# Where the background pieces of an attention stream stand within a step: behind the scores, or beside the sums of values

## The chip, the cores and the metric

The kernel runs on one NeuronCore of one Trainium2 chip. The metric is the device time of one execution in microseconds (us); lower is better. The core has engines that run side by side and each take their instructions in the order in which they were issued: TensorE (PE; its weight loads are listed as PEld), VectorE (DVE), ScalarE (ACT), GpSimd (POOL), and SyncE (SP), which here issues all DMA transfers. They wait for each other through semaphores. TensorE writes its products to PSUM, a memory of eight banks, from where VectorE and ScalarE fetch them.

## The reference

Two transformer blocks are applied in a row to `x` of 2048 tokens and 256 features, with 16 heads of 16. Cut to what matters:

```
def layer0(x, ...):                       # x0, x1: the two halves of the tokens
    x0 = x0 + gate * mha(mod(ln(x0)))     # attention inside each half   (stage 0)
    x1 = x1 + gate * mha(mod(ln(x1)))
    ox = attend(q(x0), k(x1), v(x1))      # each half looks at the other (stage 1)
    oy = attend(q(x1), k(x0), v(x0))
    x = x + gate * proj(ox, oy)
    x = x + gate * mlp(mod(ln(x)))        # 256 -> 1024 -> 256, tanh-gelu
def layer1(x, memory, mask):
    x = layernorm(x + mha(x, x, x, mask))         # 2048 x 2048 mask     (stage 2)
    x = layernorm(x + mha(x, memory, memory))     # 1601 context tokens  (stage 3)
    x = layernorm(x + relu(x @ w1 + b1) @ w2 + b2)
def attend(q, k, v):
    return softmax(q @ k.T / 4) @ v
```

## The kernel before

**Stages, units, steps.** The four attentions are four stages, and `stream` runs them as one long sequence. A stage has four blocks of 512 queries, a block four groups of four heads. One block and one group is a unit (in stage 2 the first block is cut in two parts, by keys). A unit goes over its keys in tiles of 128 with two head pairs for each, so it has two steps for every key tile: 16 steps a unit in stages 0 and 1 (1024 keys), 32 in stage 2 (16 in its first block's eight units), 26 in stage 3 (1601 keys). That makes 1440 steps. Stage 2 alone has a mask; its steps are called masked.

**What one step issues.** Four things, each on TensorE and then on another engine:
- *maxima* (`take_maxima`, `maxima`, L839): queries times keys for a unit ahead, to find each query's largest score; VectorE reduces them (L854, masked L847). There is about one such pair in a step, placed by due times (`todo`). When a unit's maxima are complete, `negated` and three steps later `as_rows` (L878, copied by ScalarE in L883) turn them into rows.
- *scores* (`second[s2]()`, which is `pair` in `weights_of`): keys times queries (L917), less the maxima (L924), in stage 2 with the mask added by a product with the identity (L932). ScalarE then takes exp of the 128 x 1024 scores (L937, the tile `e`).
- *sums* (`f()`, which is `add` in `values_of`, L953): `e` of some steps ago times the values, accumulated over a whole unit in one PSUM bank.
- *background* (`after(step)`): what is due of `later` (among it `as_rows`, `invert`, `divide`), mask tiles turned by TensorE in stage 2 (`mask_columns`, L805, copied by ScalarE in L810), one waiting transfer of keys or values, and one advance of the first background chain.

**Background chains.** All the rest of the network (projection, normalization, transposes, queries, keys, values, MLP) is written as generators, one chain for every block and stage, which advance a bit in each step. Work on TensorE is cut into pieces (`piece`): a first function issues a product into a PSUM bank, and the last one copies the result out of it. `after` starts the product. The copy is issued by `before()`, at the start of the next step:

```
if unfinished and background and not background[0][2] and background[0][1] <= now[0]:
    if not advance(background[0]):
```

In the same call the chain comes to its next piece, whose product `after` then starts in that step. So a run of pieces issues one product in each step, and every copy is issued one step after its product. Which engine copies depends on the kind of piece:

- transposes (`transposed`, L343): ScalarE (L354 or L358)
- queries and keys (`halves`, L385): ScalarE makes `hi` (L392), then VectorE `lo` (L393), which needs `hi`
- MLP up (L514): ScalarE (L522)
- values (L415), projection (L459), MLP down (L534): VectorE (L425, L477, L489)

The gelu of stage 1's MLP is taken in the first down product (L533, eight ScalarE instructions), which waits for them.

**Banks.** Six of PSUM's eight banks are three double buffers for maxima and scores (`big_ps`). The other two are `m0` and `m1`, one buffer each (`one_ps`): one holds the unit's sums, the other (`small[0]`) takes all pieces, `as_rows` and `mask_columns` of that time. The two change roles at the third step of a unit (`s2 == 2`), when `copy_sums` has ScalarE copy the finished sums (L985).

**Order.** Nothing is reordered after the program: `tc.manual_schedule` keeps every engine's instructions as issued. In an unmasked step the order on TensorE is thus maxima, sums, scores, background; in a masked one maxima, scores, sums, background. TensorE works in different tile shapes: maxima and scores use 64 rows and 128 columns (`64*128` in the profile), sums `128*32`, the mask's product and all background work `128*128`. [...]

After the last step, the last block's chain runs alone (from about 3331 us on).

Of the kernel before, what the change touches and what calls it, by code (L numbers as in the profile page):

```python
# [66 lines left out]
def slot_rows(st, slot):  # L67
    return sum(key_rows(st, n) for n in KEYS[st][slot])


def slots_of(st, b):

    return ((b // 2,), (1 - b // 2,), (0, 1), (0, 1))[st]
# [3 lines left out]
def two_layers(ctx: ExitStack, tc: tile.TileContext, a: dict, out: bass.AP):  # L77
# [583 lines left out]
    def advance(entry):  # L661

        try:
            got = next(entry[0])
        except StopIteration:
            return False
        entry[2] = got is BANK
        if got is not BANK:
            entry[1] = now[0] + got
        return True  # L670
# [190 lines left out]
    def negated(u):  # L861

        neg = sb.tile([P, TPB, 2, 2], F32, tag="neg", bufs=2, name="neg")
        nc.vector.tensor_reduce(
            neg.rearrange("p t c i -> p (t c i)"),
            u["pm"].rearrange("p t c i n -> p (t c i) n"), AX.X, ALU.max, negate=True,
        )
        v = negpad.rearrange("p t (c x) -> p t c x", c=2)
        nc.vector.tensor_copy(v[:, :, :, 0:3:2], neg)
        nc.vector.tensor_tensor(  # L870
            v[:, :, :, 1:4:2], neg, v[:, :, :, 0:3:2].bitcast(F32), ALU.subtract
        )

    def as_rows(u):

        m = one_ps()
        for qt in range(TPB):
            nc.tensor.matmul(  # L878
                m[:, qt * P : (qt + 1) * P], lhsT=negpad[:, qt, :], rhs=identR,
                start=True, stop=True,  # L880
            )
        u["nm"] = sb.tile([P, BLK], F32R, tag="nm", bufs=2, name="nm")
        nc.scalar.copy(u["nm"], m)  # L883
        if "part" in u:

            t = sb.tile([P, 2, 4 * BLK // P], F32, tag="mh", bufs=2, name="mh")
            for j in range(4):
                for h in range(2):
                    r = 64 * (j // 2) + 2 * (j % 2) + h
                    nc.sync.dma_start(  # L890
                        t[PH * j : PH * (j + 1), h, :], u["nm"][r : r + 1, :].bitcast(F32)
                    )

            def add():
                n = u["minus"] = part_tile(u, "minus")
                nc.vector.tensor_tensor(n, t[:, 0, :], t[:, 1, :], ALU.add)

            later.append([4, add, False])
# [179 lines left out]
    def stream(stages):  # L1078

        units = []  # L1080
        for st in stages:
            for b in ORDER[st]:
                blocks[st, b] = {}
                if (st, b) == (2, SPLIT):
                    units += [
                        {"st": st, "b": b, "g": g, "slots": (slot,), "part": slot}
                        for slot in range(2) for g in range(NG)
                    ]
                else:
                    units += [  # L1090
                        {"st": st, "b": b, "g": g, "slots": slots_of(st, b)} for g in range(NG)
                    ]
        for i, u in enumerate(units):
            u["i"] = i

        columns: list = []
        at = 0
        for u in units:
            steps = [(slot, kt) for slot in u["slots"] for kt in range(-(-slot_rows(u["st"], slot) // P))]
            if u["st"] == 2 and u["g"] == 0:  # L1100
                columns += [
                    (at + 2 * n - COLUMNS, u["b"], slot, kt) for n, (slot, kt) in enumerate(steps)
                ]
            u["start"], u["steps"] = at, 2 * len(steps)
            at += 2 * len(steps)

        todo: list = []
        for u, w in zip(reversed(units), [*reversed(units[:-1]), None]):
            tiles = maxima(u)
            n = len(tiles)  # L1110
            begin, length = (w["start"], w["steps"]) if w else (-n, n)
            for k in range(n - 1, -1, -1):
                due = begin + k * length / n - AHEAD
                todo.append([min(due, todo[-1][0] - SPACING) if todo else due, u, tiles[k]])

        def take_maxima(step):
            while todo and todo[-1][0] <= step:
                _, u, f = todo.pop()
                f()
                if not todo or todo[-1][1] is not u:  # L1120
                    all_maxima(u)

        def all_maxima(u):
            negated(u)
            later.append([3, lambda: as_rows(u), True])
            if u.get("part") == 0 and u["g"] == NG - 1:
                waiting.append((2, 1, 1))

        def before():

            if unfinished and background and not background[0][2] and background[0][1] <= now[0]:
                if not advance(background[0]):
                    background.pop(0)

        def after(step):

            now[0] += 1
            due = [x for x in later if x[0] <= 0]
            later[:] = [[x[0] - 1, *x[1:]] for x in later if x[0] > 0]
            for x in due:  # L1140
                x[1]()
            turned = any(x[2] for x in due)
            while columns and columns[0][0] <= step:
                mask_columns(*columns.pop(0)[1:])
                turned = True
            load_ready()
            soon = any(x[0] <= 0 and x[2] for x in later)
            soon = soon or (columns and columns[0][0] <= step + 1)
            if background and background[0][1] <= now[0]:
                if not background[0][2] or not (turned or soon):  # L1150
                    if not advance(background[0]):
                        background.pop(0)

        streaming[0] = True
        for u in units[:2]:
            load_queries(u)
        for step in range(math.floor(todo[-1][0]), 0):
            small[0] = 1
            before()
            take_maxima(step)  # L1160
            after(step)
        pending: list = []
        step = 0
        for u in units:
            i = u["i"]
            masked = u["st"] == 2
            small[0] = i % 2
            second = weights_of(u)
            for s2 in range(len(second)):
                before()  # L1170
                if s2 == 3:
                    pending += values_of(u)
                if s2 == 1 and i + 2 < len(units):
                    load_queries(units[i + 2])
                take_maxima(step)
                f = pending.pop(0) if pending else None
                if f and not masked:
                    f()
                second[s2]()

                if f and masked:
                    f()
                after(step)
                step += 1
                if s2 == 2:
                    small[0] = (i + 1) % 2
                if s2 == 2 and i:
                    w = units[i - 1]
                    copy_sums(w)
                    part = w.get("part")  # L1190
                    if part is None:
                        later.append([3, lambda w=w: invert(w), False])
                        later.append([6, lambda w=w: divide(w), False])
                    elif part == 1:
                        v = units[i - 1 - NG]
                        later.append([3, lambda w=w, v=v: compare(w, v), False])
                        later.append([4, lambda w=w, v=v: invert_both(w, v), False])
                        later.append([7, lambda w=w: (fetch_first(w), divide(w)), False])
                    if w["g"] == NG - 1 and part != 0:
                        chain_after(w)  # L1200
        small[0] = len(units) % 2
        for f in pending:
            if f:
                f()
        for x in later:
            x[1]()
        flush((0, 1))
        streaming[0] = False
        w = units[-1]
        copy_sums(w)  # L1210
        invert(w)
        divide(w)
        chain_after(w)
        while background:
            if not advance(background[0]):
                background.pop(0)
        flush((None,))
# [90 lines left out]
```

## Time and profile before

| | us |
|---|---|
| median of the runs | 3405.08 (3401.45 to 3407.21) |
| the profiled execution | 3412.04 |
| its span, first to last instruction | 3410.2 |
| ScalarE busy with exp (L937, 1440 instructions) | 1467.0 |
| PE busy with sums (L953, 10432 records) | 907.7 |
| start of stage 2's first masked score, of its last | 1272.8, 2519.5 |

How to read it: "busy" is the time in which an engine has an instruction in work; the shares of a chain are those of the way that ended last, followed back from the end. A line such as `L514` is the kernel's line, and `m_ps<-hT,w_mlp` says that the tile `m_ps` is made from `hT` and `w_mlp`. PEclk is the share of its full clock that TensorE was granted. TensorE's ends are modelled, so a matmul's length overlaps with the next one; starts are the safer reading, and below, times of TensorE's work are taken from start to start.

### The profile page before, as it was taken

Reading aid. Unit: us, or ns where it says so; the run is one execution under the profiler, and the core shown is the slowest. Engines: PE = TensorE matmul, PEld = TensorE weight load, DVE = VectorE, ACT = ScalarE, POOL = GpSimd, SP = SyncE. Lnnn points to the kernel's source line nnn. Section 1 sums busy time; section 2 is a strip of 40 time slices with the busy share of each in tenths; the row PEclk is TensorE's granted clock in tenths of the full one; section 3 lists DMA queues with packets and bytes.
Section 4 is the critical chain, followed back from the end, with each engine's and each line's share of the span. In section 5 each row is a group of like instructions: output and inputs, shape, how many; then the busy total and the mean of one; then the engine's idle time right before and its main releaser. Section 6 shows DMA issues by size and latency. Waiting matters only on the chain.

```text
span 3410.2 us, 56623 instructions
## 1 busy us (share of the span) xinstructions
PE 3088.3 (91%) x22447; PEld 1360.9 (40%) x22592; DVE 2121.6 (62%) x3858; ACT 1712.8 (50%) x1868; POOL 404.1 (12%) x344
## 2 busy tenths in 40 slices
PE   4899999999999889798999999999999999999995
PEld 2334444444443434333333333333334444444433
DVE  2676766764646365366867777777656747657541
ACT  1365655655545445243555555554555646546461
POOL 0001101101010121204013011201000011110112
PEclk8899999999999999899999999999999999999997
DMA  6652152160205221443111001102241100000000
GB/s 183 152 91 62 43 109 64 57 120 22 65 18 111 34 87 33 111 93 108 30 46 51 14 23 53 39 17 53 46 85 49 26 10 26 25 18 26 10 14 16
DMA packets 162362, 191.20 MB, mean 56 GB/s; under 512 B 82584, under 2 KB 95520, under 8 KB 162096
## 3 DMA queue, kind: packets, MB, share of 16 engines
q1 hardware_dynamic: 162096, 187.57, 22.6%
q8 instruction: 178, 2.92, 0.4%
q14 instruction: 88, 0.72, 0.1%
HBM read 129.91 MB, written 48.46 MB: 52 GB/s over the span
## 4 chain that ended last, share of the span: by engine, by line
PE 72%; DVE 8%; ACT 7%; DMA 5%; issue 3%; SPq 3%; POOL 2%; ACTq 0%; DVEq 0%; POOLq 0%
PE m_ps L953 19%; PE s_ps L917 13%; PE s_ps L839 11%; PE s_ps L924 8%; PE s_ps L932 6%; ACT e L937 6%; PE m_ps L514 3%; PE m_ps L534 3%; DVE pm L854 3%; PE m_ps L385 2%; DVE s_ps L847 2%; PE m_ps L459 2%; PE m_ps L415 2%; PE m_ps L878 1%; DVE t L328 1%
## 5 line engine op out<-in xcount | busy, mean ns | idle before, releaser
L937 ACT ACTIVATE e<-s_ps 128x1024 f32<-128x1024 f32 (+1 forms) x1440 | 1467.0, 1024 | 1387.6 <-PE s_ps L924 794.2
L854 DVE TENSOR_REDUCE pm<-s_ps 128x2 f32<-128x1024 f32 (+3 forms) x1024 | 1120.4, 1106 | 533.0 <-PE s_ps L839 528.8
L953 PE MATMUL m_ps<-e,V 128*32 128x256 f32 (+2 forms) x10432 | 907.7, 419 | 10.3 <-DVE lo L393 4.5
L847 DVE CUSTOM_DVE_ANT_0 s_ps<-s_ps,bias 128x512 f32<-128x512 f32 x1024 | 713.0, 700 | 300.4 <-PE s_ps L839 166.8
L839 PE MATMUL s_ps<-kT,q 64*128 64x512 f32 (+3 forms) x3072 | 677.1, 444 | 121.3 <-ACT e L937 51.1
L917 PE MATMUL s_ps<-q,kT 64*128 64x512 f32 (+1 forms) x2880 | 677.1, 466 | 54.0 <-ACT e L937 28.4
L924 PE MATMUL s_ps<-nm,sel 64*128 64x512 f32 (+1 forms) x2880 | 575.1, 395 | 0.1
L839 PEld LDWEIGHTS s_ps<-kT,q 64*128 64x128 f32 x3072 | 293.7, 186 | 538.6 <-issue 313.8
L917 PEld LDWEIGHTS s_ps<-q,kT 64*128 64x128 f32 (+1 forms) x2880 | 270.4, 184 | 500.4 <-issue 241.7
L953 PEld LDWEIGHTS m_ps<-e,V 128*32 128x32 f32 (+1 forms) x10432 | 207.3, 108 | 437.6 <-issue 416.0
L1031 POOL TENSOR_TENSOR oT<-oT,rd_rows 64x512 f32<-64x512 f32 x64 | 81.6, 1275 | 1902.3 <-DMA rd_rows<-rd_dr 1448.3
L932 PE MATMUL s_ps<-biasT,ident 128*128 128x512 bf16 x879 | 278.5, 385 | 23.1 <-issue 23.1
L924 PEld LDWEIGHTS s_ps<-nm,sel 64*128 64x128 f32 (+1 forms) x2880 | 275.2, 187 | 12.0 <-ACT nm L883 0.8
L782 POOL TENSOR_SCALAR bias<-raw 128x512 bf16<-128x512 int32 x64 | 123.0, 1922 | 298.4 <-DMA raw<-in_mask 276.7
L847 DVE DVE_READ_ACCUMULATOR2_ANT pm<- 128x1 f32 x1024 | 144.8, 141 | 0.0
L932 PEld LDWEIGHTS <-ident 128*128 128x128 bf16 x1024 | 58.3, 97 | 187.3 <-issue 187.3
L393 DVE SCALAR_TENSOR_TENSOR lo<-m_ps,qkb,hi 128x512 fp32r<-128x512 f32 (+2 forms) x56 | 41.1, 734 | 140.9 <-ACT hi L392 99.0
L534 PE MATMUL m_ps<-w_mlp,hid 128*128 128x256 f32 x448 | 111.2, 404 | 11.9 <-ACT hid L533 11.9
L385 PE MATMUL m_ps<-hT,w_qk 128*128 128x512 f32 (+2 forms) x224 | 111.0, 619 | 9.9 <-DVE lo L393 9.2
L514 PE MATMUL m_ps<-hT,w_mlp 128*128 128x512 f32 x224 | 111.0, 618 | 0.7 <-ACT hT L354 0.7
L534 PEld LDWEIGHTS m_ps<-w_mlp,hid 128*128 128x128 f32 x448 | 87.2, 201 | 35.4 <-ACT hid L533 14.7
L392 ACT ACTIVATE hi<-m_ps,qkb 128x512 fp32r<-128x512 f32 (+2 forms) x56 | 37.7, 674 | 82.7 <-PE m_ps L385 58.1
(106 smaller groups left out, 1233.6 us busy)
## 6 DMA issues: line engine op xcount, KB each, us to landing
q<-q_dr SPq DMA_DIRECT2D x544, 64.0 KB
kT<-k_dr SPq DMA_DIRECT2D x192, 128.0 KB
raw<-in_mask SPq DMA_DIRECT2D x64, 256.0 KB
q_dr<-hi SPq DMA_DIRECT2D x32, 256.0 KB
q_dr<-lo SPq DMA_DIRECT2D x32, 256.0 KB
oT<-sums SPq DMA_DIRECT2D x256, 32.0 KB
rd_rows<-rd_dr SPq DMA_DIRECT2D x64, 128.0 KB
v_dr<-v SPq DMA_DIRECT2D x14, 544.0 KB
```

The lines of the kernel that those rows point to most:

```text
L385: nc.tensor.matmul(m[:, :n], lhsT=wqk[:, k, w, c, :], rhs=hT[:, k, :n], start=k == 0, stop=k == 1)
L514: nc.tensor.matmul(m, lhsT=w1[k][:, f * P : (f + 1) * P], rhs=hT[:, k, :], start=k == 0, stop=k == 1,)
L534: nc.tensor.matmul(m[:, q2 * D : (q2 + 1) * D], lhsT=hid[f][:, qt * P : (qt + 1) * P], rhs=w2[f // 4][:, f % 4, :], start=f == 0, stop=f = ...
L782: nc.gpsimd.tensor_scalar(bias_rows[b, slot, qt][:, j * BLK : (j + 1) * BLK], raw, 0.0, MASKED, ALU.is_equal, ALU.mult,)
L839: nc.tensor.matmul(s[:, h, :nn], lhsT=u["q"][64 * h : 64 * h + 64, i, qt * P : (qt + 1) * P], rhs=kT[g][slot][64 * h : 64 * h + 64, i, c : ...
L847: nc.vector.tensor_tensor_reduce(out=s[:, h, :], in0=s[:, h, :], in1=bias_rows[b, slot, qt][:, c : c + nn], scale=1.0, scalar=-3.0e38, op0 ...
L854: nc.vector.tensor_reduce(u["pm"][:, qt, :, i, n], s[:, :, :nn], AX.X, ALU.max)
L917: nc.tensor.matmul(s[:r, h, :], lhsT=kT[g][slot][64 * h : 64 * h + 64, i, kt * P : kt * P + r], rhs=u["q"][64 * h : 64 * h + 64, i, :], st ...
L924: nc.tensor.matmul(s[:r, h, :], lhsT=sel[64 * h : 64 * h + 64, i, :r], rhs=u["nm"][64 * h : 64 * h + 64, :], start=False, stop=not masked,)
L932: nc.tensor.matmul(s[:, h, :], lhsT=ident16, rhs=bias_columns[b, slot, kt], start=False, stop=True,)
L937: nc.scalar.activation(e[:r], s[:r], AF.Exp, scale=SCALE)
L953: nc.tensor.matmul(u["av"][PH * j : PH * (j + 1), cut], lhsT=V[g][slot][:r, kt * GW + j * VW : kt * GW + j * VW + PH], rhs=u["e"][n, j % 2 ...
```

## The change

Within a step, the calls change places; nothing else does. Unmasked, the background now comes ahead of the sums and scores; masked, it comes between the scores and the sums.

```diff
                 take_maxima(step)
                 f = pending.pop(0) if pending else None
-                if f and not masked:
+
+
+                if masked:
+                    second[s2]()
+                after(step)
+                if f:
                     f()
-                second[s2]()
-
-                if f and masked:
-                    f()
-                after(step)
+                if not masked:
+                    second[s2]()
                 step += 1
```

The order of a step, before and after:

```
             before                                   after
unmasked     maxima, sums, scores, background         maxima, background, sums, scores
masked       maxima, scores, sums, background         maxima, scores, background, sums
```

`before()` stays at the start of a step, `take_maxima` behind it, and `copy_sums` and the switch of banks at its end.

## Prediction

> **What bounds the kernel now.** I read the page's busy table and the shares of the chain first, then the chain and the timeline inside single steps, then windows for the clock.
>
> ```profile
> PE 3088.3 (91%) x22447; PEld 1360.9 (40%) x22592; DVE 2121.6 (62%) x3858; ACT 1712.8 (50%) x1868; POOL 404.1 (12%) x344
> ...
> PE 72%; DVE 8%; ACT 7%; DMA 5%; issue 3%; SPq 3%; POOL 2%; ACTq 0%; DVEq 0%; POOLq 0%
> ```
>
> TensorE is busy 91% and holds 72% of the chain that ended last; ScalarE is half idle. So a PE instruction saved, or a PE wait added, is paid nearly in full. PE's timeline in a plain step of an unmasked stage, without background work (start, length in us):
>
> ```profile
> 504.39 0.40 PE L924 MATMUL s_ps<-nm,sel 64*128 64x512 f32 x2
> 504.62 0.40 PE L839 MATMUL s_ps<-kT,q 64*128 64x512 f32 x2
> 504.95 0.64 PE L953 MATMUL m_ps<-e,V 128*32 128x256 f32 x8
> 505.52 0.50 PE L917 MATMUL s_ps<-q,kT 64*128 64x512 f32 x2
> 505.86 0.40 PE L924 MATMUL s_ps<-nm,sel 64*128 64x512 f32 x2
> ```
>
> The scores end with L924; 0.23 us later the next maxima start (L839, the same tile shape 64*128), 0.33 later the sums of values (L953, 128*32), 0.57 later the next scores (L917), 0.34 later L924: 1.47 us. With a piece of background work, an MLP up product (L514), and then ScalarE in the same stretch (the bracket is its idle time before):
>
> ```profile
> 803.37 0.51 PE L839 MATMUL s_ps<-kT,q 64*128 64x512 f32 x2
> 803.81 0.64 PE L953 MATMUL m_ps<-e,V 128*32 128x256 f32 x8
> 804.38 0.50 PE L917 MATMUL s_ps<-q,kT 64*128 64x512 f32 x2
> 804.71 0.39 PE L924 MATMUL s_ps<-nm,sel 64*128 64x512 f32 x2
> 805.03 1.98 PE L514 MATMUL m_ps<-hT,w_mlp 128*128 128x512 f32 x4
> 806.95 0.49 PE L839 MATMUL s_ps<-kT,q 64*128 64x512 f32 x2
> ```
>
> ```profile
> 803.48 0.69 ACT L522 ACTIVATE hid<-m_ps,cols 128x512 f32<-128x512 f32 x1 [1.16 <-PE m_ps L514]
> 805.20 1.02 ACT L937 ACTIVATE e<-s_ps 128x1024 f32<-128x1024 f32 x1 [1.03 <-PE s_ps L924]
> 807.05 0.69 ACT L522 ACTIVATE hid<-m_ps,cols 128x512 f32<-128x512 f32 x1 [0.83 <-PE m_ps L514]
> ```
>
> The step takes 806.95 - 803.37 = 3.58 us, PE without a hole. Note ScalarE's order: exp of step k (L937), then the piece's copy out of its bank (L522). The exp runs beside the piece's 1.92 us; the copy then runs beside maxima, sums and scores, long before the bank's next product. Where the product in between is short, that order already shows on the chain before the change:
>
> ```profile
> 799.72 1.02 ACT e L937
> 800.74 0.68 ACT hT L354
> 801.41 0.04 issue
> 801.46 1.98 PE m_ps L514 x4
> ```
>
> PE waits there for a copy that queues behind the exp.
>
> **What the Trainium skill says.** "TensorEngine Tiling (Array Packing)", Key Properties: changing the tiling mode drains TensorE. The trace agrees: maxima after scores (both 64*128) start 0.23 us after L924, a 128*128 piece 0.32 us after it, and from maxima to sums it is 0.33 us in the plain step, 0.42 to 0.44 behind a piece. "PSUM — Partial Sum Buffer": engines must be kept off one bank by semaphores (its bank collisions section), and ScalarE's queue is strict FIFO (Engine vs sequencer instructions). The chain above is both. "TensorE: Matmul & The Clock Gate", Part 1: the clock halves after an idle window of 3.41 us on a free-running grid. Here it is harsher: a window only half busy is enough. Two windows of PE alone in stage 3 (length, busy with instructions, PEclk, DMA share and GB/s):
>
> ```profile
> 2741.90:2745.30 3.40, 1.62 (x18) 1.00 0.00 0
> 2745.30:2748.70 3.40, 3.40 (x26) 0.50 0.00 0
> ```
>
> **The change, part by part.** No instruction is added or removed; SP, POOL and VectorE keep their order, since neither scores nor sums issue DMAs, VectorE or GpSimd work. What moves: unmasked, a step was maxima, sums, scores, background and becomes maxima, background, sums, scores; masked (stage 2), maxima, scores, sums, background becomes maxima, scores, background, sums. ScalarE's order changes only unmasked: what `after` issues itself (the copy of as_rows, gelu) goes ahead of exp. The copy out of a piece's bank is issued by `before` at the next step's start, so it stays behind exp of step k.
>
> *Fewer switches.* Unmasked, scores are followed directly by maxima again, so a step with background work has one change of tile shape less. By the rows above: (0.32 + 0.43) - (0.23 + 0.33) = 0.19 us, with the middle of 0.42 and 0.44. A second reading: an up product lengthens a plain unmasked step by 3.57 - 1.48 = 2.09 us but a plain masked one, where it sits at a boundary that switches anyway, by 3.92 - 2.02 = 1.90 us; again 0.19. Masked, the mask's matmuls (L932) are 128*128 like the pieces, so one switch goes there too. Cutting PE's sequence at each first score matmul gives 224 unmasked and 143 masked steps with background work. 367 x 0.19 = 70; I take 66, because 61 of the masked ones are mask transposes (L805), which lengthen a step by only 0.33 us in all and may save about 0.12.
>
> *A wait takes their place.* Unmasked, the product of step k+1 now stands right after the maxima of k+1. Its bank (`m0` or `m1`, one per unit) is free only when the copy of piece k is done; the copy is behind exp of k, and that needs the scores of k, which now come after the product. From the start of L924: exp starts 0.49 us later and takes 1.02; the copy 0.69 more; 0.06 of handover: 2.26 us. Without a wait the product would start 0.23 + 0.33 = 0.56 us after L924. PE stands still 1.70 us, and nothing behind it can pass: sums, scores and so the next exp are queued after it. By kind of piece, counting pairs in which the very next step uses the bank or needs the data:
> - MLP up (copy L522, 0.69): 48 pairs x 1.70 = 82 us.
> - queries and keys (hi L392 0.69 on ScalarE, then lo L393 0.75 on VectorE): 1.70 + 0.75 + 0.03 = 2.48; 30 pairs, 74 us.
> - transposes (L354 0.78 or L358 0.58): 1.79 or 1.59; 17 and 9 pairs, 45 us.
> Values, projections and MLP down are copied by VectorE, which doesn't stand behind exp: their copy (0.69) ends during sums and scores (0.57 + 0.66). No wait. Small terms: gelu's three first down products wait for eight gelus anyway, about -4; four transposes at a unit's third and fourth step wait today, -7; seven first transposes at the fourth step must now wait for the copy of the sums (L985, 0.58) behind exp, +11. Sum of stalls +201 us. Masked, a whole step still lies between two products, and the copies (hi and lo 1.5 us after the product's end, against 2.0 from the start of the sums to the end of the next scores in the timeline of a stage 2 step at 1328 us) stay hidden: no cost.
>
> *The clock.* Of seven PE gaps of 1.78 us in stage 3, five were followed by a half-speed window of 3.41 us; gaps of 1.2 us brought one in about a third of cases, gaps of 1.4 us none of four. With a 1.7 us gap in every 5.1 us step I take 0.6 per gap for MLP, 0.55 for transposes, 0.85 for the 2.48 us gaps: 29 + 14 + 25 = 68 windows. One costs up to 1.7 us (half of it) when PE is busy throughout; part falls on the next gap, so I take 1.1: +75 us. Bounds: 0, since gaps of 1.13 us every 3.5 us early in stage 0 brought no slow window for 16 us, and 104 x 1.7 = +177.
>
> Sum: -66 + 201 + 75 = +210 us. Against the profiled execution (3412.0, span 3410.2) that is 3622; the runs' median, 3405.1, lies 7 lower, so 3615.
>
> **Rivals.**
> - *Stall without the clock*: -66 + 201 = +135, 3540. For it: regular short gaps kept the clock early in stage 0. Against: most gaps of 1.78 us did not.
> - *Clock down in most stalled steps*: -66 + 201 + 177 = +312, 3717. Needs every gap to count at full price.
> - *Faster: the wait is hidden.* Only the switches count: -66, 3339. Its place is the bank's release: if copies left ahead of exp, or pieces alternated banks. It decides where the mean stall per pair is below 66/104 = 0.63 us; the copy alone takes 0.58 to 0.78 us, and exp's 1.02 comes first. Against it: `one_ps` has one buffer per bank, and the chain lines show exp, copy, product in a row.
> - *No change*: switches and stalls cancel; needs just that 0.63 us.
>
> **How the numbers follow.** Stall with clock 0.62, stall alone 0.23, clock mostly down 0.08, hidden 0.05, no change 0.02. The likeliest gives 3615. The range goes from 3515 (stall alone, its 201 us some 12% smaller) to 3690 (up to two thirds of the way to the third case's clock), leaving out some 2 in 10. About 0.2% (7 us) is what a measurement here can tell from no change: faster 0.05, within 0.02, slower 0.93.
>
> **What would show it.** Right: unmasked L924 followed 0.23 us later by L839 in piece steps; MLP up steps of about 5.1 us, query and key steps of about 5.9; PE's L514, L385, L343 idle for ACT L522, DVE lo L393, ACT hT; PE's busy time no higher but for slow-clock windows in stages 0, 1 and 3; stage 2 shorter by about 24 us. Wrong: piece steps of 3.4 us without idle time before the product, or a stage 2 that grows.

## The result, and the profile after

The changed kernel takes 3588.1 us (3570.2 to 3602.2), against 3406.1 for the kernel before in the same comparison: 1.053 times as long, 95% interval 1.050 to 1.056. That is 182 us slower; 3615 with a range of 3515 to 3690 was forecast. The profiled execution took 3578.8 us, its span is 3576.7.

The page of the changed kernel, busy table and shares of the chain:

```profile
PE 3114.8 (87%) x22592; PEld 1390.5 (39%) x22592; DVE 2127.2 (59%) x3858; ACT 1701.9 (48%) x1868; POOL 404.6 (11%) x344
...
PE 68%; ACT 9%; DVE 6%; DMA 3%; issue 3%; SPq 2%; POOL 1%; ACTq 0%; POOLq 0%; DVEq 0%
```

TensorE's busy time is 27 us longer (3115 us against 3088, where the trace of before lists 145 instructions fewer) in a span that is 167 us longer: most of the time came as waiting. Its share of the chain fell from 72 to 68%, ScalarE's rose from 7 to 9%. Where in the kernel, shows in windows of PE alone, one for each group of stages: first the kernel before (stages 0 and 1, stage 2, stage 3), then the changed one (from and to, length, busy and instructions, PEclk, DMA share and GB/s):

```profile
126.60:1272.10 1145.50, 1049.34 (x7524) 0.97 0.32 71
1272.10:2521.30 1249.20, 1168.32 (x8457) 0.98 0.20 51
2521.30:3331.20 809.90, 762.17 (x6130) 0.98 0.10 28
```

```profile
125.90:1408.40 1282.50, 1069.63 (x7526) 0.94 0.27 64
1408.40:2635.20 1226.80, 1172.71 (x8603) 0.98 0.21 52
2635.20:3498.20 863.00, 764.27 (x6132) 0.96 0.10 26
```

The masked stage became 22.4 us shorter. The unmasked ones became 137 and 53 us longer, and TensorE's clock fell there. Of these 190 us, 168 are idle time of TensorE (length less busy: 144 us before, 312 after). An MLP up step of the changed kernel, TensorE (the view ends at 882.2, within the last product) and then ScalarE:

```profile
877.15 1.98 PE L514 MATMUL m_ps<-hT,w_mlp 128*128 128x512 f32 x4 [1.52 <-ACT hid L522]
879.07 0.64 PE L953 MATMUL m_ps<-e,V 128*32 128x256 f32 x8
879.64 0.50 PE L917 MATMUL s_ps<-q,kT 64*128 64x512 f32 x2
879.97 0.40 PE L924 MATMUL s_ps<-nm,sel 64*128 64x512 f32 x2
880.21 0.40 PE L839 MATMUL s_ps<-kT,q 64*128 64x512 f32 x2
882.13 0.70 PE L514 MATMUL m_ps<-hT,w_mlp 128*128 128x512 f32 x1 [1.52 <-ACT hid L522]
```

```profile
880.47 1.02 ACT L937 ACTIVATE e<-s_ps 128x1024 f32<-128x1024 f32 x1 [3.37 <-PE s_ps L924]
881.39 0.68 ACT L522 ACTIVATE hid<-m_ps,cols 128x512 f32<-128x512 f32 x1
```

Read it across: the scores end with L924 (879.97), maxima follow 0.24 us later without a switch of tile shape, then TensorE stands still until 882.13. In that gap ScalarE first takes exp of the scores just made, then, from 881.39 on, copies the piece that TensorE had left at 879.07, 2.3 us earlier. The product that waits needs the bank that this copy empties. A step takes 882.13 - 877.15 = 4.98 us; it took 3.58. The table of waits has it by line (total us, times, longest):

```profile
PE m_ps L514 <- ACT hid L522: 59.8, 39, 1.6
...
PE m_ps L385 <- DVE lo L393: 54.0, 25, 2.4
...
PE m_ps L415 <- DVE lo L393: 26.8, 12, 5.4
```

### The profile page after: what moved, and what is told of

The parts are those of the page before. It is cut to its first block, busy times and chain, and to the rows that moved or that the text cites. A ratio compares the mean times of both kernels' runs of the same rounds, so it can differ in the third digit from the quotient of the medians.

```text
span 3576.7 us, 56772 instructions
## 1 busy us (share of the span) xinstructions
PE 3114.8 (87%) x22592; PEld 1390.5 (39%) x22592; DVE 2127.2 (59%) x3858; ACT 1701.9 (48%) x1868; POOL 404.6 (11%) x344
## 4 chain that ended last, share of the span: by engine, by line
PE 68%; ACT 9%; DVE 6%; DMA 3%; issue 3%; SPq 2%; POOL 1%; ACTq 0%; POOLq 0%; DVEq 0%
PE m_ps L953 18%; PE s_ps L917 12%; PE s_ps L839 9%; PE s_ps L924 8%; PE s_ps L932 7%; ACT e L937 7%; PE m_ps L514 3%; PE m_ps L385 3%; PE m_ps L534 3%; DVE s_ps L847 2%; PE m_ps L459 2%; PE m_ps L415 1%; DVE pm L854 1%; PE m_ps L878 1%; ACT hid L522 1%
## 5 line engine op out<-in xcount | busy, mean ns | idle before, releaser
L839 PE MATMUL s_ps<-kT,q 64*128 64x512 f32 (+3 forms) x3072 | 659.9, 430 | 128.0 <-ACT e L937 59.4
L924 PE MATMUL s_ps<-nm,sel 64*128 64x512 f32 (+1 forms) x2880 | 577.3, 396 | 0.0
L932 PE MATMUL s_ps<-biasT,ident 128*128 128x512 bf16 x1024 | 311.6, 386 | 0.0
L924 PEld LDWEIGHTS s_ps<-nm,sel 64*128 64x128 f32 (+1 forms) x2880 | 277.4, 189 | 10.9 <-ACT nm L883 0.5
L385 PE MATMUL m_ps<-hT,w_qk 128*128 128x512 f32 (+2 forms) x224 | 138.7, 753 | 67.8 <-DVE lo L393 54.0
L514 PE MATMUL m_ps<-hT,w_mlp 128*128 128x512 f32 x224 | 111.9, 622 | 73.0 <-ACT hid L522 59.8
L393 DVE SCALAR_TENSOR_TENSOR lo<-m_ps,qkb,hi 128x512 fp32r<-128x512 f32 (+2 forms) x56 | 41.1, 734 | 222.5 <-ACT hi L392 206.7
L385 PEld LDWEIGHTS m_ps<-hT,w_qk 128*128 128x128 f32 x224 | 48.5, 234 | 122.7 <-DVE lo L393 64.9
```

The lines of the kernel that those rows point to most:

```text
L385: nc.tensor.matmul(m[:, :n], lhsT=wqk[:, k, w, c, :], rhs=hT[:, k, :n], start=k == 0, stop=k == 1)
L514: nc.tensor.matmul(m, lhsT=w1[k][:, f * P : (f + 1) * P], rhs=hT[:, k, :], start=k == 0, stop=k == 1,)
L839: nc.tensor.matmul(s[:, h, :nn], lhsT=u["q"][64 * h : 64 * h + 64, i, qt * P : (qt + 1) * P], rhs=kT[g][slot][64 * h : 64 * h + 64, i, c : ...
L924: nc.tensor.matmul(s[:r, h, :], lhsT=sel[64 * h : 64 * h + 64, i, :r], rhs=u["nm"][64 * h : 64 * h + 64, :], start=False, stop=not masked,)
L932: nc.tensor.matmul(s[:, h, :], lhsT=ident16, rhs=bias_columns[b, slot, kt], start=False, stop=True,)
```

## Experiments

Two theories stood against each other. The *wait theory*: a product now comes before the copy that frees its bank, because the copy is queued behind exp on ScalarE; a slower clock follows from the gaps. The rival: background ahead of the scores makes scores and exp late, whatever the copy does. "The step" in the edits is the body shown with the change.

### The two halves alone

```diff
 # e1: masked steps as changed, unmasked as before
 if masked:
     second[s2]()
+    after(step)
-after(step)
 if f:
     f()
 if not masked:
     second[s2]()
+    after(step)
```

> Masked steps as changed, unmasked steps as before. Both theories: only the switch of tile shape is saved, about 22 to 24 us in stage 2, none elsewhere: 3406 - 23 = 3383 us. If the masked half cost anything, the time would lie above 3406.

Measured: 3394.0 us, 0.995 of before (0.993 to 0.997): 12 us saved, half of what was expected. Its profile has stage 2 at 1234.9 us, 14 less than before, with 7 us more of half speed in it; the other stages moved by 4 us or less. The masked half is a gain, here smaller than the 22.4 us that the changed kernel's own profile shows.

```diff
 # e2: unmasked steps as changed, masked as before
 if masked:
     second[s2]()
+    if f:
+        f()
 after(step)
-if f:
-    f()
 if not masked:
+    if f:
+        f()
     second[s2]()
```

> Unmasked steps as changed, masked steps as before. If the two halves add up: 3588 + 23 = 3611 us, stages 0, 1 and 3 as in the changed kernel, stage 2 about 1249 us long as before. If they work on each other (clock, buffers), the sum is off by more than 15 us.

Measured: 3607.7 us, 1.059 (1.056 to 1.063), and 1249.0 us for stage 2. The run is 20 us slower than the changed kernel, a second measure of what the masked half is worth. The halves add up within some 10 us: the whole loss, and more, is in the unmasked steps.

### Background between the sums and the scores

```diff
 # e3, unmasked steps
-after(step)
 if f:
     f()
+after(step)
 second[s2]()
```

> Unmasked: sums, then background, then scores; masked as changed. Wait theory (the product waits for a copy that queues behind exp): the sums' 0.57 us now lie inside each of the 104 waits, so 59 us less, and with some slow-clock windows gone about 3515 to 3530 us; the gaps before the up products 0.95 us, before query and key products 1.75. Rival (background ahead of the scores costs because scores and exp come late, whatever the copy does): the background is still ahead of the scores, so about 3588 us.

Measured: 3502.0 us, 1.028 (1.024 to 1.031), 86 us less than the changed kernel and 13 below the lowest that was expected. The same two waits in its profile:

```profile
PE m_ps L385 <- DVE lo L393: 41.3, 25, 2.4
PE m_ps L514 <- ACT hid L522: 41.1, 39, 1.6
```

41.1 us over 39 times is 1.05 us a wait, where it was 59.8 / 39 = 1.53; for queries and keys 1.65 where it was 2.16. So a wait shrinks by about what is put in front of the waiting product, while the background still stands ahead of the scores. That speaks against the rival. Some 0.5 us in each of 104 waits is about 51 us; time at half speed fell too, from 346 us to 284, which makes up most of the rest.

### Only ScalarE's order

```diff
 # e4, unmasked steps
 after(step)
 if f:
     f()
+before()            # issues the copy of the piece that after() started
 second[s2]()
```

> As changed, but in unmasked steps the copy of a piece is issued ahead of the step's scores and exp, not at the start of the next step: TensorE's and VectorE's instructions keep exactly the changed kernel's order, ScalarE's alone differs. Wait theory: the waits before products go, the saved switches stay: 3406 - 66 = 3340 us or a little above, slow clock back to some 230 us. Rival (late scores and exp): nothing changes, about 3588 us.

Measured: 3379.1 us, 0.992 (0.989 to 0.995): 209 us faster than the changed kernel with not one TensorE or VectorE instruction moved, and faster than the kernel before. An MLP up step, TensorE, then ScalarE:

```profile
802.34 0.40 PE L924 MATMUL s_ps<-nm,sel 64*128 64x512 f32 x2
802.57 0.40 PE L839 MATMUL s_ps<-kT,q 64*128 64x512 f32 x2
802.89 1.99 PE L514 MATMUL m_ps<-hT,w_mlp 128*128 128x512 f32 x4
804.81 0.64 PE L953 MATMUL m_ps<-e,V 128*32 128x256 f32 x8
805.38 0.50 PE L917 MATMUL s_ps<-q,kT 64*128 64x512 f32 x2
805.72 0.40 PE L924 MATMUL s_ps<-nm,sel 64*128 64x512 f32 x2
```

```profile
801.53 0.69 ACT L522 ACTIVATE hid<-m_ps,cols 128x512 f32<-128x512 f32 x1 [1.06 <-PE m_ps L514]
802.84 1.02 ACT L937 ACTIVATE e<-s_ps 128x1024 f32<-128x1024 f32 x1 [0.61 <-PE s_ps L924]
804.92 0.69 ACT L522 ACTIVATE hid<-m_ps,cols 128x512 f32<-128x512 f32 x1 [1.06 <-PE m_ps L514]
```

Now the copy comes first, during the sums and scores, and exp is not late for it. The step takes 805.72 - 802.34 = 3.38 us: the 3.57 of before less the 0.19 of one switch. This settles it for the wait theory. Time at half speed is 227 us again, about what it was before the change. The run stayed 39 us above the 3340 that the theory expected; the last two runs say where some of that is. One part is plain here: a query or key piece is copied by ScalarE and then VectorE, ends 0.1 to 0.2 us too late all the same, and most of its steps take 3.55 to 3.61 us as before the change.

### The clock

The kernel before took 3409.5 us beside this run and the three after it, and 3406.1 beside the changed one, so differences to the changed kernel are good to some 4 us from here on.

```diff
 # e5, unmasked steps in which ScalarE copies a piece, first pair of maxima
-for h in range(2):
+for h in [0, 1] * (1 + again):      # again = 4 in these steps
     nc.tensor.matmul(s[:, h, :nn], ..., start=True, stop=True)
```

> As changed, but in unmasked steps in which ScalarE copies a piece, the step's first pair of maxima products is issued five times instead of once (same result, same bank): some 0.86 us more of TensorE work, which falls into the gap before the product. The waits stay as long as they are. Clock theory: gaps before query and key products shrink from 2.31 to about 1.45 us, fewer slow windows follow, slow clock falls from 346 us by 60 to 110, the time by 30 to 50, less some 10 us for copies that no product waits for: about 3550 us. Rival (slow windows fall where TensorE waits anyway and cost nothing): 3588 to 3600 us.

Measured: 3534.6 us, 1.036 (1.034 to 1.038): 54 us less than the changed kernel, with more work for TensorE. Its mean clock, and the waits (this kernel's L387 and L517 are L385 and L514 of the others):

```profile
core 0: 3523.5 us, clock 0.971
```

```profile
PE m_ps L387 <- DVE lo L396: 31.3, 25, 1.7
PE m_ps L517 <- ACT hid L526: 27.7, 39, 1.0
```

The changed kernel's clock was 0.952, with 346 us at half speed, summed from the trace's clock records; here 203 us are left, fewer even than the 233 of the kernel before, and 143 less than in the changed kernel where 60 to 110 were expected. The waits became shorter because filler stands in them, not because the copies came sooner: an up step still takes 4.98 us (the middle of 42), and all 30 steps of query and key pieces take 5.76 us, none of them at half speed. What a filled gap saves is thus the slow clock after it: 54 us net, with whatever the filler costs where no product waits.

In the changed kernel's trace the price shows directly. Queries and keys, stage 0:

```profile
455.12 1.98 PE L385 MATMUL m_ps<-hT,w_qk 128*128 128x512 f32 x4 [2.31 <-DVE lo L393]
457.03 0.64 PE L953 MATMUL m_ps<-e,V 128*32 128x256 f32 x8
457.60 0.51 PE L917 MATMUL s_ps<-q,kT 64*128 64x512 f32 x2
457.94 0.39 PE L924 MATMUL s_ps<-nm,sel 64*128 64x512 f32 x2
458.18 0.40 PE L839 MATMUL s_ps<-kT,q 64*128 64x512 f32 x2
460.88 3.62 PE L385 MATMUL m_ps<-hT,w_qk 128*128 128x512 f32 x4 [2.31 <-DVE lo L393]
464.43 0.65 PE L953 MATMUL m_ps<-e,V 128*32 128x256 f32 x8
```

Both products wait 2.31 us, but the second one takes 3.55 us from start to start instead of 1.91: it fell into 3.41 us of half speed. Such a step takes about 7.3 us (the next product starts at 468.21), one at full speed 5.76.

### Another engine for the copy

```diff
 # e6, copy of an MLP up product while the stream runs
-nc.scalar.activation(hid[f], m, AF.Identity if wait else func, bias=bias)
+if wait:
+    nc.vector.tensor_scalar(hid[f], m, bias, None, ALU.add)
+else:
+    nc.vector.tensor_scalar(hid[f], m, bias, 0.0, ALU.add, ALU.max)
```

> As changed, but the MLP up products are copied by VectorE (bias added, relu or nothing), which has no exp in its queue. Nothing else moves. Wait theory: of all gaps those of 1.52 us before the products after an up product go, 48 of them: 3588 - 73 = 3515 us, while the gaps before query and key products stay at 2.31. Rival (late scores and exp): about 3588 us.

Measured: 3514.1 us, 1.030 (1.026 to 1.033): 74 us less. In the table of waits the up products' row is gone, and that of the queries and keys is unchanged:

```profile
PE m_ps L385 <- DVE lo L393: 54.0, 25, 2.4
```

Together with the run in which only ScalarE's order changed, where ScalarE still makes the copy but ahead of exp, this shows that the place in the queue is the cause, not the engine that copies, nor the bank as such. The time at half speed stayed 347 us: these gaps of 1.52 us had brought next to none.

### What was left

```diff
 # e7: as e4, and in the third step of an unmasked unit
 before()
+if s2 == 2 and i:
+    copy_sums(units[i - 1])      # was at the step's end, behind exp
 second[s2]()
```

> As the run with the piece's copy ahead of exp, and in the third step of an unmasked unit ScalarE also copies the finished sums ahead of the step's exp. If what is left of the waits is the copy of the sums behind exp, about 11 gaps of 1.42 us go: 3379 - 16 = 3363 us. If the rest comes from elsewhere: 3379 us.

Measured: 3362.6 us, 0.986 (0.984 to 0.987), 16 us less than the run with the piece's copy ahead of exp, as expected (21 less by the ratios to the kernel before). The waits of the transposes' products, in the run before and in this one (TensorE's own and its weight loads' idle time together, times):

```profile
  ACT sums L985: 26.0, 18
```

```profile
  ACT sums L985: 3.4, 9
```

The banks change roles at the third step, so the first piece of the fourth needs the copy of the sums; that copy, too, had been behind exp.

```diff
 # e8: as e7
-go = now[0] + (9 if "part" in u else 8)
+go = now[0] + (11 if "part" in u else 10)
```

> As the run before it, and a block's chain starts two steps later, so that its first projection product, now ahead of the sums and scores, doesn't come before the division on GpSimd is done. Three such waits cost some 10 us: about 3355 us. If the later start costs as much at the end of a stage as it saves: 3363 us or more.

Measured: 3342.0 us, 0.980 (0.978 to 0.982), the fastest here: some 67 us below the kernel before in the same comparison, 246 below the changed one. The projection's wait for GpSimd's division (TensorE's and its weight loads' together again), in the run before and in this one:

```profile
  POOL oT L1031: 47.2, 13
```

```profile
  POOL oT L1031: 27.7, 5
```

Its page has TensorE at 91% of a shorter span again:

```profile
PE 3031.2 (91%) x22447; PEld 1372.2 (41%) x22592; DVE 2129.6 (64%) x3858; ACT 1711.2 (51%) x1868; POOL 404.3 (12%) x344
```

The later start saved 21 us where 8 were expected, more than the waits that it was meant for; stages 0 and 1 became 14 us shorter and stage 3 12, stage 2 10 longer. Which of the other moves brought the rest was not taken apart.

## Why the prediction was right, step by step

**Fewer switches, -66: right in kind, and about right in size.** Masked steps gave 22.4 us in the changed kernel (24 were forecast), but 12 alone in the first experiment and 20 as the difference of the second to the changed kernel. The 0.19 us of an unmasked switch stands bare once the waits are gone: 3.57 to 3.38 us. It is in the changed kernel too: its up step of 4.98 us is 3.38 and a wait of 1.60. With 224 unmasked steps that is 43 us, and 65 with the 22.4.

**The wait, +201: right in place and kind, a little too large.** From L924 to the waiting product it is 882.13 - 879.97 = 2.16 us for an MLP up product (2.26 forecast) and 460.88 - 457.94 = 2.94 for keys (3.04). The term that was off is the handover between exp and copy: the copy begins at 881.39, 0.10 us before exp's recorded end (880.47 + 1.02). Over 104 pairs that is 10 us, so about +191. The idle time of the unmasked stages, a second reading, grew by 168 us; it is net of waits that some of these products had before the change already, and of the other small moves. That pieces copied by VectorE don't wait held too: moving the up products' copies there removed their wait.

**The clock, +75: right in kind, too large, and in part put on the wrong pieces.** Time at half speed grew from 233 to 346 us, by 33 windows of 3.41 us, not 68; a window cost 7.3 - 5.76 = 1.5 us, not 1.1. That makes some 51 us. The two errors partly cancel, so that the size came out as near as it did is in part luck. The filler run fits: it took away 143 us of half speed, 42 windows, which at 1.5 us is 63, and saved 54 net. The step that failed is the chance of 0.6 for each gap before an up product: of the 42 products with such a gap that stand right behind another up product, one met a half-speed window that began between the start of its gap and 3.4 us after its own. By the same count it was 21 of the 30 products right behind a query or key piece (25 forecast), and 13 of the 26 behind a transpose (14 forecast); before the change the three counts were 0, 2 and 0, which leaves the 33. (The remaining 6 of the 48 up pairs end in a down product; 3 of these met one, before the change and after.)

**The sum.** -65 + 191 + 51 = +177 us, beside 182 measured on the medians and 167 between the two profiled spans. Of the rivals, the faster one would have needed the copy ahead of exp; the fourth experiment made just that, and is faster. The stall without the clock (3540) is what the filler run comes near, at 3535, though with some 9 half-speed windows fewer than the kernel before.

## What to carry to other kernels

Before a product is moved forward within a step, ask which copy frees its bank, on which queue that copy stands, and what it stands behind; a saved 0.19 us on the busiest engine bought a wait of 1.5 to 2.3 us because the copy's place in another engine's queue was not moved along. The cure was to move the copy, not to undo the move. And a gap on TensorE had a second price here, the slow clock after it: it came where gaps filled about half of a window of 3.41 us or more.

## What was unexpected

How well TensorE's busy share tells when the clock falls. Cut on the grid on which the slow stretches begin, into windows of 3.413 us from the start of the stream to its end, the full-speed windows of the two kernels sort like this by TensorE's busy share (the number of windows, and how many were followed by one at half speed):

| busy share of the window | before | changed |
|---|---|---|
| under 0.50 | 16, 15 slow | 42, 41 slow |
| 0.50 to 0.60 | 13, 9 slow | 63, 13 slow |
| over 0.60 | 869, none | 808, 1 slow |

The Trainium skill ("TensorE: Matmul & The Clock Gate", Part 1) says that the clock halves after at least one idle window of about 3.4 us; in these traces a window that was half idle was enough, nearly always. The edge isn't a sharp line: in the run with the background between sums and scores, 9 of 35 windows under 0.50 were not followed by a slow one, all nine at 0.45 to 0.50.

The length of a gap alone doesn't decide. One gap of 1.52 us in a step of 4.97, as before the up products, leaves a window of 3.41 us some 55% busy, and brought a slow one in 1 of 42 cases; one gap of 2.31 us leaves it a third busy, and did so in 21 of 30. But behind transposes, where the gaps were 1.33 to 1.62 us, 13 of 26 products met one, all 13 in steps of 3.0 to 4.2 us and none of the three in steps of 5.7. That fits gaps that come closer together, so that a window holds parts of two of them; this reading was not tested by a run of its own.
